# A four-layer vision network on one core: attention's keys in column groups, its first maxima earlier, and layer 2 begun with the values

## The chip, the cores and the metric

The kernel runs on one core of a Trainium2 chip, as one launch for a batch of four images. The metric is the device time of the launch in microseconds (us); lower is better. Each time below is that of the whole launch.

## The reference

Four images of 256 channels and 64 x 64 points pass through four layers one after the other; each layer adds its output to its input, and reads its input normalised over groups of 8 channels:

```python
x = x + deform_conv(gn(x))      # layer 0: 3x3 deformable convolution
x = x + attention(gn(x))        # layer 1
x = x + dcnv4(gn(x))            # layer 2
x = x + mamba(gn(x))            # layer 3: a selective scan
```

Two of the layers matter here. Layer 1, with N = 4096 points:

```python
q = xf @ Wq.T + bq              # 32 channels
k = xf @ Wk.T + bk              # 32 channels
v = relu(xf @ Wv.T + bv)        # 128 channels
attn = softmax(q @ k.T)         # 4096 x 4096 for each image
comb = (attn @ v) @ Wc.T + bc
out = concatenate([comb, v])
```

Layer 2 samples a value map `xp = x @ w_value + b_value`, padded by one point, at nine learned offsets for each of 16 groups, weighs the samples with a learned mask, and projects the sum:

```python
val = w00*g(y0,x0) + w01*g(y0,x0+1) + w10*g(y0+1,x0) + w11*g(y0+1,x0+1)
out = einsum('bhwkgc,bhwgk->bhwgc', val, mask)
```

## The kernel before

The input `x` of one image stays in SBUF as 2 x 128 channels on 128 partitions, and all four layers work on it in place. The images follow one another; in each of them the layers follow one another, since a layer's normalisation needs the statistics of the whole image. The order of a stage's instructions is written out by hand for the engines that `tc.manual_schedule` names; for the other engines, and for the DMA queue of SyncE (SP), a planner orders the instructions from its own estimate of when each will be ready. Within an engine instructions run strictly in that order.

**Layer 1 (`layer1`).** `scaled` (L186, VectorE) writes the normalised input `xn` in sixteen pieces of 128 x 512. Then comes a part that is called the front here (L485 to L519), in which only TensorE's order is by hand. It goes over eight chunks `j` of 512 points. For each chunk three products of 128 x 512 are made: values `pv`, keys `pk`, queries `pq` (all on L499; each is two matrix products over 128 channels, and each of these is two instructions[...]). The weights of keys and queries hold the same 32 columns four times side by side, so that the 32 rows of `pq` and of `pk` stand on all four groups of 32 partitions. Queries are kept that way in `qa` (L506). Of the keys, a chunk keeps one group of 32 rows only (L505): chunk `j` goes to the partitions of group `j % 4` and to half `j // 4` of `ka`, so that later four products with a contraction of 32 rows run in the four row groups of the array at once. The values are turned into rows of points by four transposes (`pvt`, L509) and kept in `v`; they are also added to `x` (L516), and the next layer's statistics of that chunk are taken (L152).

The softmax subtracts each query's greatest score before the exponential. `greatest(qb, wide, n)` finds the greatest of all 4096 scores for each of the 512 queries of block `qb`. It makes 32 score tiles of 128 x 512 (L455), `n` at a time into one PSUM tile, and reduces them with VectorE (L465); a generator's `yield` after each step lets the caller place it in TensorE's order. Then it splits the maxima into three bf16 parts (L472 to L475), turns them into a row with four small products (`pmt`, L479), and copies the row to SBUF (`mr`, L483). In the front it is called for block 0 with `n = 2` and two PSUM tiles of two banks: after each odd chunk four steps, and after the last chunk also the closing part. In the attention loop behind it (`scores`, `weigh`) it is called with `n = 3` for the blocks 1 to 7, each while the block before is worked on. The loop starts with `scores(0)`, which needs the row of block 0; its exponentials are L544.

**Layer 2 (`layer2`).** `scaled` writes the normalised input into `xr` (L186 again, 20 pieces of 256 to 512 columns), laid out as two halves of the image side by side. The loop then goes over 16 pairs of rows `p`. The values of rows are held in a ring of four tiles (`ring`, 128 x 2560, L690 to L692): `values(q)` makes two rows of values with TensorE (`pc`, L702 and L704), copies them into the middle of ring tile `q % 4` with ScalarE (L705), and lets eight DMAs of SP's queue copy them, shifted by one and two columns to either side, into the four other places (L709). Places at the image's edge that no DMA writes must be zero, so GpSimd clears each ring tile at the layer's start (L691). `offsets` (L720, L723) makes offsets and mask, `hats`, `masked` and `outer` make bilinear weights from them, `clear` and `gather` add these into a table `A` of 5 x 5 weights, `product` (L823) multiplies the ring with it, and `total` (L840) sums on TensorE. Row `p` needs ring tiles `p` to `p + 2`. From the line `with tc.manual_schedule` in `layer2` on, the order is by hand for TensorE, ScalarE, VectorE and GpSimd; the four clearings of the ring stand ahead of it, so the planner places them.

Of the kernel before, what the change touches and what calls it, by code (L numbers as in the profile page):

```python
# [9 lines left out]
F32 = mybir.dt.float32  # L10
I32 = mybir.dt.int32
BF16 = mybir.dt.bfloat16
AF = mybir.ActivationFunctionType
ALU = mybir.AluOpType
AX = mybir.AxisListType

P = 128
# [42 lines left out]
WIN = 5  # L60
VR = 2


class Net:
# [346 lines left out]
    def layer1(self, x):  # L411
# [4 lines left out]
        with tc.tile_pool(name="l1a", bufs=1) as pa, tc.tile_pool(name="l1b", bufs=2) as pb:  # L416
# [24 lines left out]
            def greatest(qb, wide, n):  # L441


                m8 = pb.tile([P, 4, 8], F32, tag="m8", name="m8")
                m = m8.rearrange("p t m -> p (t m)")
                if n == 2:
                    units = [(t, c, g) for c in range(2) for h in range(2) for t in range(4) for g in (2 * h, 2 * h + 1)]
                else:
                    units = [(t, c, g) for t in range(4) for c in range(2) for g in range(4)]
                for u in range(0, 32, n):  # L450
                    now = units[u : u + n]
                    sc = wide("pm")
                    for i, (t, c, g) in enumerate(now):
                        r = slice(32 * g, 32 * g + 32)
                        nc.tensor.matmul(  # L455
                            sc[:, i, :],
                            qa[r, bass.ts(4 * qb + t, P)],
                            ka[r, bass.ts(c, 512)],
                            start=True,
                            stop=True,  # L460
                            tile_position=(32 * g, 0),
                        )
                    t, c, g = now[0]
                    at = 8 * t + 4 * c + g
                    nc.vector.tensor_reduce(m[:, at : at + len(now)], sc[:, : len(now), :], AX.X, ALU.max)  # L465
                    yield
                mx = pb.tile([P, 4], F32, tag="mx", name="mx")
                nc.vector.tensor_reduce(mx, m8, AX.X, ALU.max, negate=True)
                mp = parts[qb % 2]
                for i in range(3):  # L470
                    t3 = pb.tile([P, 4], BF16, tag="t3", name="t3")
                    nc.scalar.copy(t3, mx)  # L472
                    nc.scalar.copy(mp[:, :, :, i], t3.rearrange("p (t u) -> p t u", u=1).to_broadcast([P, 4, 4]))
                    if i < 2:
                        nc.vector.tensor_sub(mx, mx, t3)  # L475
                yield
                pt = wide("pmt")[:, 0, :]
                for t in range(4):
                    nc.tensor.matmul(  # L479
                        pt[:, bass.ts(t, P)], mp[:, t].rearrange("p g r -> p (g r)"), identb, start=True, stop=True  # L480
                    )
                mr = pb.tile([P, 512], BF16, tag="mr", name="mr")
                nc.vector.tensor_copy(mr, pt)  # L483
                rows.append(mr)

            with (
                tc.manual_schedule(engines={mybir.EngineType.PE}),
                self.banks(4, "l1p") as pone,
                self.banks(2, "l1w") as ptwo,
            ):  # L490
                pair = lambda name: ptwo.tile([P, 2, 512], F32, tag="pm", name=name)
                one = lambda name: pone.tile([P, 512], F32, tag="p", name=name)
                ahead = greatest(0, pair, 2)
                for j in range(NCH):
                    to = {}
                    for n, w in (("v", wv), ("k", wk), ("q", wq)):
                        to[n] = one("p" + n)
                        for ct in range(2):
                            nc.tensor.matmul(  # L499
                                to[n], w[:, ct, :], xn[:, ct, bass.ts(j, 512)], start=(ct == 0), stop=(ct == 1)  # L500
                            )
                    vt = pb.tile([P, 512], F32, tag="vt1", name="vt1")
                    nc.vector.tensor_scalar(vt, to["v"], bv, 0.0, ALU.add, ALU.max)
                    r = slice(32 * (j % 4), 32 * (j % 4) + 32)
                    nc.scalar.activation(ka[r, bass.ts(j // 4, 512)], to["k"][r, :], AF.Identity, bias=bk[r])  # L505
                    nc.scalar.activation(qa[:, bass.ts(j, 512)], to["q"], AF.Identity, bias=bq)  # L506
                    pt = one("pvt")
                    for i in range(4):
                        nc.tensor.transpose(pt[:, bass.ts(i, P)], vt[:, bass.ts(i, P)], self.ident)  # L509
                    nc.scalar.copy(v[:, 4 * j : 4 * j + 4, :].rearrange("p t c -> p (t c)"), pt)  # L510

                    if j % 2:
                        for _ in range(4):
                            next(ahead)
                    xs = x[:, 1, bass.ts(j, 512)]
                    nc.vector.tensor_add(xs, xs, vt)  # L516
                    self.note(x, 1, j)
                next(ahead)
                next(ahead, None)  # L519

            blocks = [{} for _ in range(NCH)]
# [131 lines left out]
    def layer2(self, x):  # L653
# [5 lines left out]
        with (  # L659
# [28 lines left out]
            for i in range(4):  # L688

                r = pa.tile([P, WIN, VR, 256], F32, tag=f"ring{i}", name=f"ring{i}")  # L690
                nc.gpsimd.memset(r, 0.0)  # L691
                ring.append(r)  # L692

            def values(q):
# [156 lines left out]
            with tc.manual_schedule(  # L851
                engines={
                    mybir.EngineType.PE,
                    mybir.EngineType.Activation,
                    mybir.EngineType.DVE,
                    mybir.EngineType.Pool,
                }
            ):
                for t in range(T):
                    offsets(0, t)  # L860
                hats(0, 0)
                hats(0, 1)
                clear(0)
                values(0)
                masked(0)
                for i in range(3):
                    outer(0, i, nc.gpsimd if i == 1 else nc.vector)
                values(1)
                values(2)
                for t in range(T):  # L870
                    offsets(1, t)
                for i in (0, 2, 1):
                    gather(0, i)
                hats(1, 0)
                hats(1, 1)


                behind = None
                for p in range(last + 1):
                    near, far = p < last, p < last - 1  # L880
                    for wy in range(WIN):
                        product(p, wy, 0)
                        if near and wy == 0:
                            masked(p + 1)
                        product(p, wy, 1)
                        if wy == 1 and p > 1:
                            finish(p - 2)
                        if near and wy > 1:
                            gather(p + 1, wy - 2)
                        if near and wy < 3:  # L890
                            outer(p + 1, wy, nc.gpsimd)
                        prod = pairs(p)
                        if behind:
                            total(*behind)
                        behind = p, wy, prod
                        if wy == 0:
                            if near:
                                clear(p + 1)
                            if p:
                                nc.scalar.copy(made[p - 1]["o"].rearrange("p t c -> p (t c)"), made[p - 1]["pd"])  # L900
                        if far and wy < 2:
                            offsets(p + 2, wy)
                        if wy == 2:
                            if far:
                                hats(p + 2, 0)
                            if p < last:
                                values(p + 3)
                        if wy == 3:
                            if far:
                                hats(p + 2, 1)  # L910
                            if p:
                                turned(p - 1)
                        if wy == 4 and p:
                            project(p - 1)
                total(*behind)
                nc.scalar.copy(made[last]["o"].rearrange("p t c -> p (t c)"), made[last]["pd"])
                finish(last - 1)
                turned(last)
                project(last)
                finish(last)  # L920
# [710 lines left out]
```

## Time and profile before

| what | value |
|---|---|
| median of the runs shown | 10109.86 us (10098.28 to 10119.21) |
| the profiled execution | 10144.41 us, of which its span is 10142.6 us |
| mean granted TensorE clock | 0.95 of full speed |
| TensorE busy | 8738.3 us, 86% of the span |
| VectorE busy | 7651.8 us, 75% |
| GpSimd busy | 6768.8 us, 67% |
| ScalarE busy | 4961.6 us, 49% |

In the first image the stages that matter lie as follows (us from the span's start). The others look the same, some 2500 us apart.

| stage | from | to | length |
|---|---|---|---|
| front of layer 1, from the first piece of `xn` to the first exponential | 634.2 | 713.3 | 79.1 |
| attention loop, first to last exponential | 713.3 | 1148.3 | 435.0 |
| end of layer 1 and start of layer 2, to the first product with the ring | 1148.3 | 1198.2 | 49.9 |
| layer 2's loop | 1198.2 | 1545.7 | 347.5 |

Busy shares are means over stages with different limits. What an edit in one stage is worth is read from that stage: from who waits for whom in it, and from which wait ends last.

### The profile page before, as it was taken

How to read it: one execution, taken by the hardware profiler on the slowest of the kernel's cores; microseconds unless marked ns; L12 is line 12 of the kernel's file. 1: busy time of each engine (PE TensorE's matmuls, PEld its weight loads, DVE VectorE, ACT ScalarE, POOL GpSimd, SP SyncE). 2: the span in 40 equal slices, each digit the busy share in tenths (PEclk: the TensorE clock that was granted, in tenths of full speed). 3: DMA queues.
4: the chain of work that ended last, by engine and by line, in shares of the span. 5: the costliest groups of instructions: out<-in, count | busy, mean ns of one | idle time of the engine just before them, and what ended most of it. 6: DMA issues, size and time to landing. Idle time of an engine off the chain costs nothing.

```text
span 10142.6 us, 88824 instructions
## 1 busy us (share of the span) xinstructions
PE 8738.3 (86%) x29189; PEld 4281.7 (42%) x29193; DVE 7651.8 (75%) x8215; ACT 4961.6 (49%) x7588; POOL 6768.8 (67%) x3952
## 2 busy tenths in 40 slices
PE   5789898998678989899877898989986789998997
PEld 3643343333464334333346434433334643443333
DVE  5764497999676459799967545889995754688998
ACT  3743334665474333566557333266645733326664
POOL 3646686787474668688757366768865736677886
PEclk9889999999899999999989999999998999999999
DMA  7830011111783001111178201111118810111111
GB/s 263 310 137 1 25 49 39 44 45 48 259 312 119 1 29 49 38 44 47 45 287 323 78 1 36 51 38 44 44 43 316 308 62 1 38 49 38 40 40 34
DMA packets 377891, 956.56 MB, mean 94 GB/s; under 512 B 34675, under 2 KB 107820, under 8 KB 375372
## 3 DMA queue, kind: packets, MB, share of 16 engines
q0 software_dynamic: 165888, 604.05, 16.6%
q1 hardware_dynamic: 211532, 346.73, 10.8%
q8 instruction: 234, 3.83, 0.2%
q14 instruction: 237, 1.94, 0.1%
HBM read 784.59 MB, written 92.32 MB: 86 GB/s over the span
## 4 chain that ended last, share of the span: by engine, by line
PE 24%; DVE 9%; ACT 5%; issue 4%; POOL 4%; DMA 3%; another core or an unknown queue 1%; SPq 0%; POOLq 0%; DVEq 0%; ACTq 0%
PE cx L555 5%; DVE h L1476 4%; PE pacc L840 3%; PE y L1388 2%; DMA g<-tab,idx 2%; PE pm L455 2%; PE front L1236 2%; POOL h L1490 2%; DVE h L1468 2%; PE sc L531 2%; PE front L1190 1%; ACT da L1475 1%; DVE r L353 1%; POOL g L344 1%; DMA ring<-ring 1%
## 5 line engine op out<-in xcount | busy, mean ns | idle before, releaser
L1476 DVE TENSOR_TENSOR_SCAN h<-da,carry,h 128x512 f32<-128x512 f32 x2048 | 2470.6, 1264 | 140.9 <-ACT da L1475 92.5
L1490 POOL TENSOR_TENSOR h<-h,cn 128x2048 f32<-128x2048 f32 x508 | 2300.0, 4527 | 41.1 <-POOL carry L1487 0.4
L1475 ACT ACTIVATE da<-delta,l3a 128x512 f32<-128x512 f32 x2048 | 1388.6, 689 | 1152.5 <-DVE h L1476 1150.7
L1388 PE MATMUL y<-h,ident 128*128 128x512 f32 x4096 | 1931.4, 616 | 4.5 <-POOL h L1490 3.5
L344 POOL DMA_INDIRECT g<-tab,idx x1152 | 1363.3, 1183 | 791.1 <-issue 362.8
L548 POOL TENSOR_TENSOR acc<-acc,e 128x1024 f32<-128x1024 f32 x480 | 1125.1, 2344 | 540.4 <-ACT e L544 519.7
L388 PE MATMUL pz<-cols,l0w 128*128 128x256 f32 x4608 | 1217.5, 411 | 219.8 <-ACT cols L377 95.8
L1388 PEld LDWEIGHTS y<-h,ident 128*128 128x128 f32 x4096 | 810.2, 198 | 1279.3 <-issue 1209.7
L353 DVE SCALAR_TENSOR_TENSOR r<-g,wx,r 128x512 f32<-128x512 f32 x1152 | 858.1, 745 | 434.3 <-ACT r L352 321.9
L1468 DVE TENSOR_TENSOR h<-du,bn 128x2048 f32<-128x2048 f32 x512 | 1157.9, 2262 | 26.3 <-PE front L1190 14.2
L465 DVE TENSOR_REDUCE m<-pm 128x3 f32<-128x1536 f32 (+1 forms) x372 | 602.3, 1625 | 716.9 <-PE pm L455 715.2
L388 PEld LDWEIGHTS pz<-cols,l0w 128*128 128x128 f32 x4608 | 896.9, 205 | 390.7 <-ACT cols L377 100.9
L823 DVE TENSOR_TENSOR prod<-ring,A 128x1280 f32<-128x1280 f32 x640 | 922.4, 1480 | 122.7 <-DMA ring<-ring 102.7
L555 PE MATMUL cx<-e,v 128*128 128x512 f32 x2048 | 1001.4, 616 | 0.0
L544 ACT ACTIVATE e<-sc 128x1024 f32<-128x1024 f32 x512 | 496.0, 1020 | 1032.4 <-PE sc L531 1032.4
L352 ACT ACTIVATE r<-g,wx 128x512 f32<-128x512 f32 x1152 | 826.6, 718 | 270.0 <-DMA g<-tab,idx 219.2
L840 PE MATMUL pacc<-prod,ident 128*128 128x512 f32 x1920 | 915.3, 610 | 37.7 <-DVE prod L823 23.7
L832 POOL TENSOR_TENSOR prod<-prod 128x512 f32<-128x512 f32 x640 | 800.3, 1274 | 187.8 <-DVE prod L823 170.1
L370 PE MATMUL pt<-ident,acc 128*128 128x128 f32 x2304 | 430.9, 295 | 304.9 <-DVE acc L361 200.7
L1487 POOL COPY carry<-h 128x4 f32<-128x4 f32 x512 | 98.0, 191 | 807.4 <-DVE h L1476 797.6
L555 PEld LDWEIGHTS cx<-e,v 128*128 128x128 f32 x2048 | 352.2, 189 | 598.8 <-issue 596.3
L360 ACT ACTIVATE acc<-r,wy 128x256 f32<-128x256 f32 x1152 | 571.4, 496 | 28.0 <-DVE r L353 22.4
(250 smaller groups left out, 11138.0 us busy)
## 6 DMA issues: line engine op xcount, KB each, us to landing
cn<-cd SPq DMA_DIRECT2D x512, 256.0 KB
tab<-vt SPq DMA_DIRECT2D x112, 640.0 KB
ring<-ring SPq DMA_DIRECT2D x288, 126.0 KB
ring<-ring SPq DMA_DIRECT2D x288, 124.0 KB
g<-tab,idx POOLq DMA_INDIRECT x1152
x<-in_x SPq DMA_DIRECT2D x64, 256.0 KB
out<-x SPq DMA_DIRECT2D x56, 256.0 KB
l0w<-in_l0w SPq DMA_DIRECT2D x4, 2304.0 KB
```

The costliest lines, as they stand in the source:

```text
L344: nc.gpsimd.indirect_dma_start(out=g[:], out_offset=None, in_=tab[:, :], in_offset=bass.IndirectOffsetOnAxis(ap=idx[:, t, k : k + 1], axis=0),
L353: nc.vector.scalar_tensor_tensor(r, g[:, :, 1, :], wx[:, 1, t, k : k + 1], r, ALU.mult, ALU.add)
L388: nc.tensor.matmul(sums[m][:, ot, :256], wf[:, i, bass.ts(ot, P)], cols[m][:, i, :], start=(i == 0), stop=(i == 17),)
L548: nc.gpsimd.tensor_add(b["acc"], b["acc"], e)
L555: nc.tensor.matmul(blocks[qb]["cx"], v[:, 4 * (i + kt // 4 * 4) + kt % 4, :], e[:, bass.ts(i % 2, 512)], start=(kt == 0 and i == 0), stop= ...
L823: nc.vector.tensor_mul(d["prod"][:, :, t, :].rearrange("p x (g c) -> p x g c", c=GC), ring[y // VR % 4][:, :, y % VR, :].rearrange("p x (g ...
L840: nc.tensor.matmul(d["pd"], self.ident, prod[:, wx, :], start=(wy == 0 and wx == 4), stop=(wy == WIN - 1 and wx == 2),)
L1388: nc.tensor.matmul(c["ys"][dc], self.ident, h[:, dc, :], start=False, stop=(n == DS - 1))
L1468: nc.vector.tensor_mul(h, c["du"], c.pop(("bn", n)).to_broadcast([P, 4, C]))
L1475: nc.scalar.activation(da, c["delta"][:, dc, :], AF.Exp, scale=al[:, dc, n : n + 1])
L1476: nc.vector.tensor_tensor_scan(h[:, dc, :], da, h[:, dc, :], carry[:, dc, n : n + 1], ALU.mult, ALU.add)
L1490: nc.gpsimd.tensor_mul(h, h, cn.to_broadcast([P, 4, C]))
```

## The change

In layer 1's front, the keys of four chunks are made together: `keys(c)` takes only 32 columns of the weights and lets four products run side by side in the four column groups of the array, each writing its own 32 partitions of one PSUM tile; one copy of 128 x 512 then fills half of `ka`. The maxima of block 0 are made four tiles at a time (one PSUM tile of four banks in place of two of two banks), in the same order as in the loop, and they are placed between the chunks from chunk 1 on, with the closing part in chunks 6 and 7. A small exponential of a constant (`tiny1`) stands ahead of the front. In layer 2 GpSimd clears ring tiles 0 and 1 at the start, ScalarE clears tile 2, and GpSimd clears tile 3 inside the hand-written order; `values(0)` stands ahead of the first `offsets`, `values(1)` ahead of the first `masked`, and `values(2)` behind the second pair of `offsets`.

```diff
--- before.py
+++ after.py
@@ -443,10 +443,7 @@
 
                 m8 = pb.tile([P, 4, 8], F32, tag="m8", name="m8")
                 m = m8.rearrange("p t m -> p (t m)")
-                if n == 2:
-                    units = [(t, c, g) for c in range(2) for h in range(2) for t in range(4) for g in (2 * h, 2 * h + 1)]
-                else:
-                    units = [(t, c, g) for t in range(4) for c in range(2) for g in range(4)]
+                units = [(t, c, g) for t in range(4) for c in range(2) for g in range(4)]
                 for u in range(0, 32, n):
                     now = units[u : u + n]
                     sc = wide("pm")
@@ -486,36 +483,56 @@
             with (
                 tc.manual_schedule(engines={mybir.EngineType.PE}),
                 self.banks(4, "l1p") as pone,
-                self.banks(2, "l1w") as ptwo,
+                self.banks(1, "l1w") as pfour,
             ):
-                pair = lambda name: ptwo.tile([P, 2, 512], F32, tag="pm", name=name)
+                four = lambda name: pfour.tile([P, 4, 512], F32, tag="pm", name=name)
                 one = lambda name: pone.tile([P, 512], F32, tag="p", name=name)
-                ahead = greatest(0, pair, 2)
+
+                tiny = pa.tile([P, 1], F32, tag="tiny1", name="tiny1")
+                nc.scalar.activation(tiny, self.eps, AF.Exp)
+
+                def keys(c):
+
+                    pk = one("pk")
+                    for ct in range(2):
+                        for g in range(4):
+                            nc.tensor.matmul(
+                                pk[32 * g : 32 * g + 32, :],
+                                wk[:, ct, :32],
+                                xn[:, ct, bass.ts(4 * c + g, 512)],
+                                start=(ct == 0),
+                                stop=(ct == 1),
+                                tile_position=(0, 32 * g),
+                            )
+                    nc.scalar.activation(ka[:, bass.ts(c, 512)], pk, AF.Identity, bias=bk)
+
+                def project(n, w, j):
+                    to = one("p" + n)
+                    for ct in range(2):
+                        nc.tensor.matmul(to, w[:, ct, :], xn[:, ct, bass.ts(j, 512)], start=(ct == 0), stop=(ct == 1))
+                    return to
+
+
+                ahead = greatest(0, four, 4)
                 for j in range(NCH):
-                    to = {}
-                    for n, w in (("v", wv), ("k", wk), ("q", wq)):
-                        to[n] = one("p" + n)
-                        for ct in range(2):
-                            nc.tensor.matmul(
-                                to[n], w[:, ct, :], xn[:, ct, bass.ts(j, 512)], start=(ct == 0), stop=(ct == 1)
-                            )
+                    pv = project("v", wv, j)
                     vt = pb.tile([P, 512], F32, tag="vt1", name="vt1")
-                    nc.vector.tensor_scalar(vt, to["v"], bv, 0.0, ALU.add, ALU.max)
-                    r = slice(32 * (j % 4), 32 * (j % 4) + 32)
-                    nc.scalar.activation(ka[r, bass.ts(j // 4, 512)], to["k"][r, :], AF.Identity, bias=bk[r])
-                    nc.scalar.activation(qa[:, bass.ts(j, 512)], to["q"], AF.Identity, bias=bq)
+                    nc.vector.tensor_scalar(vt, pv, bv, 0.0, ALU.add, ALU.max)
+                    if j > 1:
+                        next(ahead, None)
+                    pq = project("q", wq, j)
+                    nc.scalar.activation(qa[:, bass.ts(j, 512)], pq, AF.Identity, bias=bq)
+                    if j < 2:
+                        keys(j)
+                    if j in (1, 3, 5, 6):
+                        next(ahead)
                     pt = one("pvt")
                     for i in range(4):
                         nc.tensor.transpose(pt[:, bass.ts(i, P)], vt[:, bass.ts(i, P)], self.ident)
                     nc.scalar.copy(v[:, 4 * j : 4 * j + 4, :].rearrange("p t c -> p (t c)"), pt)
-
-                    if j % 2:
-                        for _ in range(4):
-                            next(ahead)
                     xs = x[:, 1, bass.ts(j, 512)]
                     nc.vector.tensor_add(xs, xs, vt)
                     self.note(x, 1, j)
-                next(ahead)
                 next(ahead, None)
 
             blocks = [{} for _ in range(NCH)]
@@ -688,7 +705,12 @@
             for i in range(4):
 
                 r = pa.tile([P, WIN, VR, 256], F32, tag=f"ring{i}", name=f"ring{i}")
-                nc.gpsimd.memset(r, 0.0)
+                if i < 2:
+                    nc.gpsimd.memset(r, 0.0)
+                elif i == 2:
+                    nc.scalar.copy(
+                        r.rearrange("p x y c -> p (x y c)"), zero.to_broadcast([P, WIN * VR * 256])
+                    )
                 ring.append(r)
 
             def values(q):
@@ -856,19 +878,20 @@
                     mybir.EngineType.Pool,
                 }
             ):
+                values(0)
                 for t in range(T):
                     offsets(0, t)
                 hats(0, 0)
                 hats(0, 1)
                 clear(0)
-                values(0)
+                values(1)
                 masked(0)
                 for i in range(3):
                     outer(0, i, nc.gpsimd if i == 1 else nc.vector)
-                values(1)
-                values(2)
                 for t in range(T):
                     offsets(1, t)
+                nc.gpsimd.memset(ring[3], 0.0)
+                values(2)
                 for i in (0, 2, 1):
                     gather(0, i)
                 hats(1, 0)
```

## The prediction

> **What bounds the kernel now.** I read the page first: TensorE is busy for 86% of the span and no other engine for more than 75%, but these are means, so I went to the stages. The view of busy time by stretches, for the front of layer 1, the attention loop, the start of layer 2 and layer 2's loop (length, then busy time of PE, PEld, DVE, ACT and POOL, granted clock, DMA share, GB/s):
>
> ```profile
> 634.20:713.30 79.10, 73.52 (x208) 30.74 (x208) 44.98 (x61) 17.19 (x31) 0.00 (x0) 0.87 0.00 0
> 713.30:1148.30 435.00, 424.21 (x1915) 164.25 (x1916) 176.25 (x133) 136.57 (x177) 285.64 (x127) 0.99 0.00 1
> 1148.30:1198.20 49.90, 33.48 (x92) 17.27 (x90) 23.76 (x42) 12.60 (x17) 16.40 (x13) 0.69 0.16 51
> 1198.20:1545.70 347.50, 334.74 (x935) 161.37 (x936) 318.41 (x352) 107.04 (x164) 274.82 (x203) 0.99 0.16 49
> ```
>
> The front is TensorE's, at 0.87 of its clock; the start of layer 2 is nobody's. The chain of waits, in order of time, shows the front of image 4 (start, length, what):
>
> ```profile
> 8191.28 1.11 PE pm L455 x4
> 8192.41 1.24 DVE m L465
> 8193.69 1.13 PE pm L455 x4
> 8194.82 1.13 PE pm L455 x4
> 8195.95 1.92 PE pv L499 x4
> 8197.87 1.72 PE pk L499 x4
> 8199.58 1.72 PE pq L499 x4
> 8201.30 0.44 PE pvt L509 x4
> ```
>
> So the path runs through every projection, 1.72 us each, and passes to VectorE only where four steps of maxima come at once. The same view at the start of layer 2, image 3:
>
> ```profile
> 6190.72 3.22 PE pom L720 x4
> ...
> 6201.06 0.72 ACT A L756
> 6201.78 0.52 ACT ring L705
> ...
> 6209.31 9.35 DMA ring<-ring
> 6218.67 12.36 DMA ring<-ring
> 6231.05 12.21 DMA ring<-ring
> ```
>
> Offsets come first, then ScalarE's weights, then the copy of `values(0)`, and three ring tiles' DMAs, one after the other. What comes ahead of that is in the order of time of image 1 (start, length, what):
>
> ```profile
> 1160.53 8.88 POOL L691 MEMSET ring<- 128x2560 f32 x4
> 1165.79 4.46 DVE L186 TENSOR_SCALAR xr<-x,gm,rs 128x256 f32<-128x256 f32 x4
> ```
>
> Four pieces of `xr` take 4.46 us, although a piece of 128x512 takes 533 ns in the table by shape: the clearing lies over them, and ends at 1169.41.
>
> [...] layer 0's convolution in this form (L280) issues 144 instructions in 15.66 us, 0.109 us each, against 0.43 us for one of `pk`. [...] The first two pieces above end only with the third and the fourth clearing. [...] The front's clock records show windows of 3.41 us at 0.50: one behind each of the first two groups of four maxima, two behind the third. [...] Ring DMAs have 62 or 63[...]; the 62-row ones follow each other at 2.5 us in the trace's landings, and a ring tile takes 12.2 us.
>
> **Part 1, layer 1's front, per image.** From the first `pv` (634.84) to the first exponential (713.31): 78.5 us.
> - Keys: 8 x 4 x 0.43 = 13.8 us become 2 x 16 x 0.109 = 3.5. On TensorE's path: -10.3. ScalarE's eight copies (678 ns) become two of some 688 ns (the row of `qa`), hidden beside TensorE.
> - Maxima: 16 steps of 0.86 us (two of the four row groups at work) become 8 of 0.97 (the loop's eight instructions of `sc` start 0.97 ahead of what follows). -6.0.
> - VectorE's waits inside the four groups: four steps take 4.67 us in the chain above, for 3.44 of matmul. -1.2 x 4 = -4.9.
> - Half clock behind them: four windows of 3.41 us, half lost. -6.8.
> - The tail: after the last maxima (four steps, ending at 708.4) the row of block 0 still needs the split, `pmt` and `mr`, 4.9 us to the first exponential. Now the row is ready ahead of it; `scores(0)` waits for the last copies of `qa` and `v`, and takes 1.3: 2.5 in all. -2.4.
> - New waits: the PSUM tile of four banks is single, so a step waits for the reduction before it. By 1024 in 1.22 and 1536 in 1.757 us, 2048 take 2.3. Between most steps TensorE has 3.9 us of other work; behind it are queued the next projections, and the chunk's transposes wait in turn for VectorE's `vt`. In chunks 3 and 5, with two steps each, only `pq` (1.72) lies between: some 1.35 us each; with 0.35 in four other places and 0.5 for `pmt`, +4.6. One of these stops may cost a window at half clock: +1.7, taken half, 0.9.
> VectorE has 7.4 (`xn`) + 8 x 2.15 + 8 x 2.3 + 1 = 44 us of work in it, TensorE 31.0 + 3.5 + 7.8 + 0.3 = 42.6 and a cold start of 2.9: both nearly full, the new length some 53 us. Sum: 30.4 - 5.5 = **-25**. Bounds: -30 if the new waits vanish; -17 if VectorE's order, which the planner sets, puts sums and statistics ahead of reductions and each step stops for another microsecond. The little exponential only moves a table load of 1.28 us; the old one was hidden by `mr`. If the planner puts it ahead of the square root, the load returns beside the last `v` copy: 0 to +1.3, taken 0.
>
> **Part 2, start of layer 2, per image.** T is the first ring DMA: 1181.48 in image 1, 15.7 us after the first piece of `xr` (1165.79); 16 to 17 in the others.
> - The clearing: two memsets (2.23 each) from 1160.53 end at 1165.0, ahead of `xr`. `values(0)` needs the first two pieces: 0.4 each (20 pieces without the overlap follow at 0.46), so TensorE starts near 1166.4.
> - `values(0)`: two rows at the half clock, 2.3 each as at 1181.5, 4.7; copy and hand-over 0.8. T becomes 1171.9: **-9.6**, and some 10 over the four images.
> - Behind it on TensorE the first offsets start 4.7 later than their pieces allow, near 1171 against 1170.03, so `hats` hardly move. ScalarE has `hats` and the clear of `A` ahead of the copy of `values(1)`, so that comes near 1181.5, T + 9.6, where before the ninth DMA went out at T + 7.3. The two engines then still have rows until T + 16.3: hidden. `values(2)` stands behind `offsets(1)`, which waits for `masked(0)` to free its banks, near 1180.5; the copy comes near 1191, T + 19, as before (1200.38). All eight DMAs of each tile keep their order on SP's queue, and the queue is bound by the 62-row transfers, so all three tiles land earlier by the shift of T.
> - `gather(0)` ends near 1188.5, level with tile 0; the products before tile 1 have 3 us to spare.
> - ScalarE's clear: 800 elements take 842 ns (`A`), so 2560 some 2.7 us, between 1160.6 and the square root's load at 1163.92. Cover 0.6 us; if the planner puts it late, at most 2.7 on the path of `rs`. GpSimd's clear of tile 3 (2.23) lies between its `outer` and its first `pairs`, which waits for tile 0: hidden, and without that cover 2.2.
> Bounds: -11.5 to -5. Layer 2's loop is TensorE's from the third tile on, so the shift stays. In both parts removed work cannot slow TensorE's order itself; a loss could come only through the clock or the planner, below.
>
> **Sum.** 4 x 25 + 4 x 10 = 140 us. The profiled execution would go from 10144.4 to 10004; it lies 34 us above the median, and I take the difference off the median: 10109.86 - 140 = **9970**.
>
> **Rivals.**
> 1. *VectorE sets the front's pace* (13%): every step stops TensorE for a reduction and what the planner put ahead of it. For it: 44 us of work on VectorE in a front of 53. Against it: the loop does just this with three tiles, stops 0.8 us a step, and keeps a clock of 0.99. At -12 an image, with layer 2's 10, -88: 10022.
> 2. *Layer 2's start gains only part* (9%): tile 2 comes late because of `values(2)`, or the clearing of tile 2 delays the square root. At -3 an image: 9998.
> 3. *The column groups do not overlap* (3%): the change does not do what it says of the keys, 2 x 16 x 0.43 = 13.8 as before. Against it is L280. -15 and -10 an image: 10010.
> 4. *Slower* (3%): the front falls to half clock and stays there, since each of eight steps ends in a full stop of 2.3 us on the single PSUM tile. 42.6 x 2 + 18.4 + 2.5 = 106 us, +28 an image, less 10: 10182. It decides from a front of 89 us on. The clock fell behind each group of maxima before; but those used half the row groups, and the loop's stops never lowered it.
>
> **How the numbers follow.** The likeliest case has 72%. The bounds, 4 x (17 to 30) and 4 x (5 to 11.5), give -88 to -166, 9944 to 10022. They hold rivals 2 and 3 and the edge of 1. I say 9942 to 10020. About 0.2%, 20 us, is what a measurement of this kernel can tell from no change: faster 0.95, same 0.02, slower 0.03.
>
> **What would show it.** Right: the front takes 50 to 58 us; `po`-like products of `pk`, 32 instructions at 0.11 us; eight reductions of 128x2048 at 2.3 us; no gap between the last `pvt` and `sc` but for a copy; the first pieces of `xr` at 0.4 us each; the first ring DMA 6 us after them, and three tiles still at 12.2 us each. Wrong: a front over 65 us with a clock below 0.85 (step of new waits), or a third tile that lands less than 6 us sooner after `xr` (part 2).

## The result, and the profile after

| what | before | after |
|---|---|---|
| median | 10104.07 us (4 runs, 10093.64 to 10119.21) | 9973.85 us (4 runs, 9971.41 to 9981.35) |
| ratio | 1 | 0.9871, 95% interval 0.9854 to 0.9888 |
| profiled execution | 10144.41 us (span 10142.6) | 9981.35 us (span 9979.5) |

The change saves 130.2 us, where 140 were forecast. In one of 25 executions of the kernel before, in a later series, the granted clock was 0.82 and the time 10876.27 us; medians and ratios below leave it out. The two profiled executions differ by 163.1 us of span, which is more than the change gives. Setting the stages of the four images against each other in the two traces:

| stage, sum over four images | before | after | difference |
|---|---|---|---|
| front of layer 1, first `xn` to first exponential | 314.2 | 228.0 | -86.2 |
| attention loop and its end | 1783.8 | 1785.5 | +1.7 |
| last addition of layer 1 to the product that waits for the third ring tile | 253.0 | 209.4 | -43.6 |
| rest of layer 2 and start of layer 3 | 1574.4 | 1583.4 | +9.0 |
| the rest of layers 0 and 3, and the end | 6217.1 | 6173.2 | -43.9 |

The two stages that were edited give -129.8, the difference of the medians. The last row has no edited line in it; over all the traces of this study, of whatever kernel, it lies between 6173.2 and 6230.9 us, so a difference of 43.9 is within what one trace differs from another. Nearly all of the +9.0 is a window at half clock of 10.2 us that falls at layer 3's start in two of the four images of this trace, at 4.2 us each; another execution of the same kernel has it in one.

The view of busy time by stretches after the change, image 1 (length, then busy time of PE, PEld, DVE, ACT and POOL, granted clock, DMA share, GB/s), the same four stages as before:

```profile
619.90:676.80 56.90, 49.83 (x208) 19.42 (x208) 43.55 (x53) 13.46 (x25) 0.00 (x0) 0.95 0.00 0
676.80:1112.00 435.20, 424.82 (x1915) 164.48 (x1916) 176.23 (x133) 136.59 (x178) 285.59 (x127) 0.99 0.00 1
1112.00:1152.60 40.60, 32.34 (x92) 16.15 (x90) 20.70 (x43) 12.50 (x16) 19.88 (x12) 0.75 0.21 66
1152.60:1498.50 345.90, 333.95 (x936) 161.74 (x935) 318.35 (x352) 109.25 (x166) 274.81 (x203) 0.98 0.16 49
```

In the front PE falls by 24 us at the same count of instructions (208), VectorE's work stays (44.98 to 43.55), and the clock rises from 0.87 to 0.95. The loops keep their lengths within 2 us. The groups by shape in that front (line, engine, operation, shapes, count, busy, mean ns, idle before), maxima and keys before, and then after the change:

```profile
L455 PE MATMUL pm<-ka,qa 32*128 32x512 f32 x64 | 18.0, 659 | 2.0 <-DVE m L465 2.0
L499 PE MATMUL pk<-xn,l 128*128 128x512 f32 x32 | 17.1, 662 | 0.0
```

```profile
L462 DVE TENSOR_REDUCE m<-pm 128x4 f32<-128x2048 f32 x8 | 18.2, 2280 | 5.0 <-PE pm L452 5.0
...
L452 PE MATMUL pm<-ka,qa 32*128 32x512 f32 x64 | 9.1, 639 | 3.4 <-DVE m L462 3.2
L499 PE MATMUL pk<-xn,l 128*32 128x512 f32 x32 | 3.8, 598 | 0.0
L561 ACT ACT_TABLE_LOAD x1 | 1.3, 1283 | 1.5 <-issue 1.5
```

32 instructions of keys in four column groups have TensorE busy for 3.8 us, where the 32 before took 17.1: a mean of 598 ns each, yet 0.12 us apiece, since four run side by side. The 64 of maxima take 9.1 instead of 18.0. The reduction of four banks takes 2.28 us. The last line is the load of ScalarE's function table between the first scores and the first exponential, on the path. Before, it ran beside `mr`, to 712.64, and the exponential came at 713.31:

```profile
711.36 1.28 ACT L544 ACT_TABLE_LOAD   x1
711.90 0.69 DVE L483 CAST mr<-pmt 128x512 bf16<-128x512 f32 x1 [1.09 <-PE pmt L479]
```

The chain of waits at the start of layer 2, image 4 (start, length, what):

```profile
8549.65 2.32 ACT ring L711
8551.99 1.28 ACT L175
...
8553.85 0.42 DVE xr L186
...
8554.52 2.04 PE pc L724 x4
...
8556.89 1.80 PE pc L724 x4
...
8558.99 0.59 ACT ring L727
...
8566.22 10.09 DMA ring<-ring
8576.32 12.29 DMA ring<-ring
8588.63 12.22 DMA ring<-ring
```

Offsets, hats and the clearing of `A`, which stood in the chain before, are gone from it: one piece of `xr`, two rows of values, one copy, and then the DMAs, still 12.2 us a tile. ScalarE's own clearing stands at its head. The groups by shape around it, image 1:

```profile
L186 DVE TENSOR_SCALAR xr<-x,gm,rs 128x256 f32<-128x256 f32 x4 | 1.4, 408 | 0.1
L709 POOL MEMSET ring<- 128x2560 f32 x2 | 4.4, 2231 | 0.0
L1078 POOL TENSOR_SCALAR l3a<-l3a 128x64 f32<-128x64 f32 x1 | 6.1, 6117 | 2.4 <-ACT l3a L1077 2.4
```

Nothing lies over the pieces of `xr` now, so four take 1.4 us in place of 4.46.

### The profile page after: what moved, and what is told of

It is laid out like the page before. It is cut to its first block, busy times and chain, and to the rows that moved or that the text cites. A ratio compares the mean times of both kernels' runs of the same rounds, so it can differ in the third digit from the quotient of the medians.

```text
span 9979.5 us, 88756 instructions
## 1 busy us (share of the span) xinstructions
PE 8624.9 (86%) x29193; PEld 4231.9 (42%) x29193; DVE 7632.5 (76%) x8183; ACT 4959.9 (50%) x7576; POOL 6758.0 (68%) x3948
## 5 line engine op out<-in xcount | busy, mean ns | idle before, releaser
L462 DVE TENSOR_REDUCE m<-pm 128x3 f32<-128x1536 f32 (+2 forms) x340 | 599.3, 1763 | 699.7 <-PE pm L452 699.7
L561 ACT ACTIVATE e<-sc 128x1024 f32<-128x1024 f32 x512 | 496.0, 1020 | 1029.7 <-PE sc L548 1029.7
L845 DVE TENSOR_TENSOR prod<-ring,A 128x1280 f32<-128x1280 f32 x640 | 922.6, 1480 | 79.1 <-DMA ring<-ring 60.8
```

The costliest lines, as they stand in the source:

```text
L845: nc.vector.tensor_mul(d["prod"][:, :, t, :].rearrange("p x (g c) -> p x g c", c=GC), ring[y // VR % 4][:, :, y % VR, :].rearrange("p x (g ...
```

## The experiments

Each was measured beside the kernel before: the first four on one chip, the next four on a second, the last four on a third. The kernel before had medians of 10136.55, 10116.06 and 10144.68 us there, so totals are compared on one chip, or as ratios. The changed kernel was run on the third of these chips alone: on the first two it stands only by its ratio of the first measurement, 0.9871 (0.9854 to 0.9888), and against it differences below some 20 us can't be told by time. Stage times are sums over four images in the profiled execution, worked out from the starts in the trace.

**Each part alone.** The changed kernel with layer 2 as before:

```diff
-                values(0)
                 for t in range(T):
                     offsets(0, t)
...
-                values(1)
+                values(0)
                 masked(0)
...
+                values(1)
+                values(2)
                 for t in range(T):
                     offsets(1, t)
-                nc.gpsimd.memset(ring[3], 0.0)
-                values(2)
```

(and all four clearings on GpSimd, as before).

> Layer 1's part of the change alone, layer 2 as before. If the two parts are independent, the front shortens by some 21.5 us an image as in the profile of the whole change, so 86 us less than before, some 10018, and layer 2's start keeps its 63 us. If the parts need each other, or if a part of the 130 us came from layer 0 (whose transfers differ from run to run), it lies above 10035.

10045.07 us, ratio 0.9909 (0.9896 to 0.9923): -91.5, where 86 were expected; that the time itself is above the 10035 is this chip's, on which the kernel before takes 32 us more than in the first measurement. Front 227.4 us; start of layer 2 253.4, as before.

And the kernel before with layer 2's edits only, the same lines the other way round:

> Layer 2's part of the change alone, layer 1 as before. Independent parts: 11 us an image between the last addition of layer 1 and the product that waits for the third ring tile, 44 us in all, some 10060. If the windows at half clock at the start of layer 3, which two of four images showed in the profile of the whole change and none before, come with the shift of layer 2, up to 9 us of that are lost: 10069.

10092.25 us, ratio 0.9951 (0.9937 to 0.9965): -44.3. Front 315.8, start of layer 2 208.2. The start of layer 3 shows no long window here (70.9 to 71.6 us in the four images), so the shift of layer 2 alone need not bring it. The two parts add up to 135.8, against 139.2 for both together on the third chip (below) and 130.2 in the first measurement: they are independent within what the times can tell.

**Keys alone.** The kernel before with keys in four column groups; maxima in pairs, at their old places:

```diff
-                    for n, w in (("v", wv), ("k", wk), ("q", wq)):
+                    for n, w in (("v", wv), ("q", wq)):
...
+                    if j < 2:
+                        keys(j)
```

> Only the keys: made for four chunks in four column groups in chunks 0 and 1; the maxima of block 0 stay in pairs, four steps behind each odd chunk, and the tail stays. By the prediction's sum this takes 10.3 us an image off TensorE's order and leaves the 4.9 of waits, the 6.8 of half clock and the tail: -41 us, some 10063, a front of 68.5 us with three or four windows at half clock. Rival: with less work between the groups of maxima the clock falls more often, so that the gain is below 8 us an image.

10101.33 us, ratio 0.9968 (0.9956 to 0.9980): -35.2; front 275.2, so -39.0, or 9.8 an image. Stretches, image 1, of this front, and then of the run with the whole front:

```profile
624.00:693.60 69.60, 64.06 (x208) 25.32 (x208) 45.00 (x61) 13.13 (x25) 0.00 (x0) 0.84 0.00 0
```

```profile
623.30:680.20 56.90, 49.73 (x208) 19.41 (x208) 43.55 (x53) 13.51 (x26) 0.00 (x0) 0.95 0.00 0
```

With keys alone the clock is even lower than before, 0.84, but the windows at half clock are as many as before, four of 3.41 us in image 1, and stand where the groups of maxima are; the rival's fall of the clock did not come. They go with the early maxima of four tiles, which take the other 12 us of an image (275.2 to 227.4 over four). TensorE was not idle ahead of these windows: in the 3.41 us before each run of them in the front, in every image of the kernel before, it was busy for 2.9 us, with maxima and at most one other instruction. That a stop of TensorE brings such a window, on which the prediction's 0.9 us and its rival 4 rested, was the author's assumption, and these windows do not show it. The change does two things to these maxima at once: it has four row groups at work in place of two, and it breaks up the groups of four steps. Which of the two removes the windows was not tried.

**The table load.** The changed kernel with its small exponential reading `xn`, so that it comes behind the square root:

```diff
-                nc.scalar.activation(tiny, self.eps, AF.Exp)
+                nc.scalar.activation(tiny, xn[:, 0, 0:1], AF.Exp)
```

> The whole change, but the little exponential reads the first piece of xn in place of the constant, so that it can't run ahead of the square root. Theory: in the changed kernel its table is displaced by the square root's, and the load of 1.28 us stands between the first scores and the first exponential, behind a wait; here it moves into ScalarE's idle time at the front's start, 1.3 us less an image, 5 us below the changed kernel (9969), and a front of 55.6 us. Rival: the load is not on the path (the row or the PSUM copy ends last), no change within 0.05%. If the window at half clock at the start of the loop comes from this stop, it goes as well, another 1 to 2 us an image.

Front 221.9 us, 6.1 less than 228.0: 1.5 an image. The total, 9986.96 us, has ratio 0.9857 (0.9841 to 0.9873), which does not part from the changed kernel's 0.9871. The window at half clock at the start of the loop, which the expectation suspected of the load, stays in all four images (3.4 to 6.8 us). Table loads by shape, of the changed kernel and then of this one, from layer 0's end to the first exponentials:

```profile
L492 ACT ACT_TABLE_LOAD x1 | 1.3, 1283 | 2.9 <-PE pz L388 2.9
L175 ACT ACT_TABLE_LOAD x1 | 1.3, 1283 | 2.9 <-PE pv L173 2.9
L561 ACT ACT_TABLE_LOAD x1 | 1.3, 1283 | 1.5 <-issue 1.5
```

```profile
L175 ACT ACT_TABLE_LOAD x1 | 1.3, 1283 | 7.5 <-PE pv L173 7.5
L492 ACT ACT_TABLE_LOAD x1 | 1.3, 1283 | 0.9 <-DVE xn L186 0.9
```

In the changed kernel three loads are made: the planner put `tiny1`, which waits for nothing late, ahead of the square root (L175), which loads its own table over it; the exponential (L561) pays again, on the path. With an input that comes late there are two, and none at L561.

**Order without spread.** The changed kernel with all four clearings on GpSimd ahead of `xr`:

```diff
-                if i < 2:
-                    nc.gpsimd.memset(r, 0.0)
-                elif i == 2:
-                    nc.scalar.copy(
...
+                nc.gpsimd.memset(r, 0.0)
...
-                nc.gpsimd.memset(ring[3], 0.0)
```

> The changed kernel with all four clearings of ring tiles put back on GpSimd ahead of the first normalized value; the values still come before the offsets. My theory: of layer 2's gain of 10.9 us an image, the order gives most and the spread of the clearing only part. With four clearings GpSimd is at work for some 13 us, so the pieces of the normalized array on VectorE run beside it (2.6 us instead of 0.41 for the first), and ScalarE has nothing between the exponential and the square root, so the 1.28 us table load stands on the path again: from the last addition of layer 1 to the product that waits for the third ring tile 52.3 us grow to some 56 to 57, 16 to 20 us over the changed kernel for four images, still 24 to 28 us under the kernel before in this stretch. Rival: the spread is what gives the gain (the values would have been held up by the clearing anyway): then nearly all of the 44 us are lost. Second rival: the clearing is hidden, and the time is that of the changed kernel within 5 us.

9996.50 us, ratio 0.9882 (0.9867 to 0.9898), which the times alone do not part from the changed kernel; the stretch (from the last addition of layer 1 to the product that waits for the third ring tile) 222.1, 12.7 more than the changed kernel, somewhat less than the 16 to 20 expected. The four clearings take 8.9 us, not the 13 of the expectation. The chain of image 4:

```profile
8574.42 1.28 ACT L175
8576.28 3.77 DVE xr L186 x2
8580.19 1.19 PE pc L719 x2
8581.71 2.00 PE pc L719 x4
```

Two pieces of `xr` take 3.77 us on the path. The price an image is 2.4 us there (8.45 from first piece to first ring DMA, against 6.0) and 0.9 ahead of it (5.97 from the last addition to the first piece, against 5.0 to 5.3).

**Spread without order.** The kernel before with the clearing spread only; its diff is the corresponding part of the change.

> The kernel before with the clearing of the ring's tiles spread alone: tile 2 on ScalarE, tile 3 on GpSimd later; the offsets stay ahead of the values. My theory: the pieces of the normalized array come some 3 us earlier and the square root's table load may slip out of the path (1.3 us), but the offsets ahead of the values still take their time, so the stretch from the last addition to the third tile's product falls from 63.2 to some 59 us an image: about 12 to 17 us less than the kernel before. Together with the run that has the order alone the two should give about 44 us. Rival: the order of the instructions is all, and the spread gives nothing (0 to 3 us).

10093.52 us (21 runs), ratio 0.9978 (0.9971 to 0.9984): -22.5; the stretch 235.9, 17.1 less than before. The chain of image 4, where the offsets still come first:

```profile
8658.33 3.13 PE pom L725 x4
...
8663.71 1.22 ACT hat L740
8664.93 1.05 ACT hat L741
...
8668.52 0.72 ACT A L761
8669.24 0.52 ACT ring L710
```

Order alone saves 253.0 - 222.1 = 30.9, the spread alone 17.1, both 43.6: the order gives more, but each is worth something without the other, and none of the rivals in the two expectations holds. Singly they sum to 48.0, so 4.4 of it is gained by either one.

**What sets the ring's 12.2 us.** The changed kernel with each transfer of 62 rows cut in two:

```diff
-                        nc.sync.dma_start(out=r[a:b, 2 + d, :, :], in_=r[a + d : b + d, 2, :, :])
+                        for c0, c1 in ((a, a + 60), (a + 60, b)) if abs(d) == 2 else ((a, b),):
+                            nc.sync.dma_start(out=r[c0:c1, 2 + d, :, :], in_=r[c0 + d : c1 + d, 2, :, :])
```

> The changed kernel with each ring transfer of 62 rows cut into 60 rows and 2 rows. In the changed kernel a ring tile's four copies end 12.2 us after each other, and the theory puts this down to the 62-row transfers[...]. If so, the third tile lands some 15 to 25 us earlier, and the stretch from the last addition of layer 1 to its product (52.3 us an image) gets shorter by 4 to 10 us until the next thing ends last (the gather's offsets and weights, or the values of tile 2 on TensorE at half clock): 15 to 40 us less in all, and up to 10 us more at the end of layer 2 where the last rows' copies are waited for. Rival: the queue of the issuing engine or what comes after it sets the pace (eight more issues a tile row at some 0.7 us each): no gain, or some us slower.

9951.00 us, ratio 0.9841 (0.9826 to 0.9857); the stretch 176.1, 33.3 less than the changed kernel or 8.3 an image. The DMA view in 40 slices, busy share of the 16 engines in tenths and GB/s, of the changed kernel (1130 to 1175 us) and of this one (1135 to 1165 us):

```profile
DMA  0000012443421111344321111124541111111111
GB/s 0 0 0 0 7 16 80 102 144 87 126 78 51 51 51 51 118 144 157 115 75 51 51 51 49 46 67 153 171 162 66 51 51 51 66 49 53 51 49 36
```

```profile
DMA  0000040413444633200140414444615040404444
GB/s 0 0 0 0 0 158 11 137 33 117 131 137 142 199 131 112 57 0 0 46 123 36 134 33 156 128 145 139 224 46 156 0 164 5 161 19 139 131 153 134
```

The plateaus at 51 GB/s are the 62-row transfers (124 KB at one landing in 2.5 us are 51 GB/s); in the second view they are gone. From 1144 to 1148 us, in the first plateau, the engines' share is 13.2%, the time of 2.1 of the 16; over the whole of the two views it is 21.0% in the first and 28.8% in the second. On how many engines one transfer lies is not shown. The issuing queue did not set the pace, though it has four issues more for each ring tile (four of the eight transfers have 62 rows; the expectation's eight is wrong). The products with the ring, in the costliest groups of the page, changed kernel and then this one:

```profile
L845 DVE TENSOR_TENSOR prod<-ring,A 128x1280 f32<-128x1280 f32 x640 | 922.6, 1480 | 79.1 <-DMA ring<-ring 60.8
```

```profile
L846 DVE TENSOR_TENSOR prod<-ring,A 128x1280 f32<-128x1280 f32 x640 | 919.7, 1481 | 40.2 <-PE pacc L863 37.6
```

DMAs no longer end most of VectorE's waits for these products; TensorE does. At the start of layer 2 VectorE now waits for ScalarE's hats, made from the offsets (image 1: total, times, longest):

```profile
DVE mh L769 <- ACT hat L762: 9.6, 2, 6.6
```

So what the change put behind `values(0)` ends last there, as the expectation named it. Whether another order is better with cut transfers was not tried. The hoped-for gain at the loop's end didn't come: from the third tile's product to the last one takes 323.0 us in image 1, as with uncut transfers (323.1). The waits for the last rows there were off the path.

**An addition on GpSimd.** The changed kernel with the front's `x` additions moved from VectorE:

```diff
-                    nc.vector.tensor_add(xs, xs, vt)
+                    nc.gpsimd.tensor_add(xs, xs, vt)
```

> The changed kernel with the eight additions of the front (x plus the attention values) on GpSimd, which is idle there, instead of VectorE. VectorE is at work for 43.6 of the front's 56.9 us, and two maxima in chunks 3 and 5 wait for it for some 0.4 us each beyond the spacing of 1.07. If VectorE's load makes these stalls, the front gets shorter by 0.8 to 2 us an image (3 to 8 us in all, about what can be measured). Rival: [...] the additions cost more on GpSimd than they free: the last one stands ahead of the first scores' operands, so the front gets longer by 1 to 3 us an image. Second rival: nothing moves, since the stalls are TensorE's own.

9989.97 us, ratio 0.9878 (0.9863 to 0.9893), not parted from the changed kernel by time; front 238.1, 10.1 longer, or 2.5 an image, which is a length that the first rival gave (1 to 3). But the trace shows a wait that no theory had named:

```profile
DVE st L152 <- POOL x L534: 10.0, 8, 1.4
```

(waits in image 1's front: total, times, longest). The addition takes 1.26 us on GpSimd instead of 0.69, and the chunk's statistics, which VectorE takes in order ahead of other work, wait for it eight times. The reductions behind them come later, and TensorE's stops for reductions grow from 3.2 to 4.4 us in image 1 (its front from 56.9 to 58.2). Work was taken off VectorE, but the wait stayed in its queue. Statistics and reductions themselves take as long as before (0.69 and 2.28 us), so nothing shows VectorE held up; since it stands idle for most of each addition (10.0 of 10.1 us), whether the two engines would hold each other up can't be told from this run.

**The changed kernel again, and VectorE's order.** First the changed kernel on the third chip:

> The changed kernel itself once more, so that the kernels beside it can be set against it on one chip. 0.985 to 0.989 of the kernel before. The front is 56.3 to 57.4 us an image and the stretch from the last addition of layer 1 to the third ring tile's product 52.3 us, as in its first profile.

10005.47 us, ratio 0.9867 (0.9852 to 0.9882): -139.2; front 227.2, stretch 209.4. Beside it, the changed kernel with VectorE's front in the written order:

```diff
-                tc.manual_schedule(engines={mybir.EngineType.PE}),
+                tc.manual_schedule(engines={mybir.EngineType.PE, mybir.EngineType.DVE}),
```

> The changed kernel with VectorE's instructions of the front kept in the written order too. In the changed kernel the planner puts the addition and the statistics of a chunk (0.69 us each) ahead of the maxima's reduction, which is 1.2 us late by it in chunks 3, 5 and 6; the next maxima find their one buffer of four banks taken, which is the 1.50 us idle time seen twice in an image. In the written order the reduction goes first. My theory: the two idle times fall from 1.50 to some 0.6 us (a maxima unit and its reduction, 1.07 and 2.28 and a handover, against 2.92 us of maxima and projection), and the last row of maxima comes 0.8 us earlier: front 2 to 2.6 us shorter an image, 8 to 10 us in all. Rival: the addition and statistics then delay VectorE's next copy of the values by 1.4 us, the transposes behind it wait, and the front stays as it is or grows by up to 1 us an image.

Front 217.6, 9.6 less than beside it, as the theory had it. TensorE's waits for the reductions in image 1's front, of the changed kernel and then of this one:

```profile
PE pm L452 <- DVE m L462: 3.2, 3, 1.5
```

```profile
PE pm L452 <- DVE m L462: 1.2, 3, 0.5
```

But the total is 10005.66 us (ratio 0.9866, 0.9851 to 0.9881), no gain at all. Layers 0 and 3 took 12.0 us more in this trace than in the one beside it, within the 58 us over which they vary. A gain of 9.6 in 10000 us stands in the trace and is below what the times resolve here; whether it reaches the total stays open.

**The best version.** The small exponential and the cut transfers together, and then with VectorE's order as well:

> The changed kernel with two edits together: the small exponential that reads the normalized array (table load off the path, 1.5 us an image) and the ring transfers of 62 rows cut into 60 and 2 (8.3 us an image). If the two are independent: 36 to 40 us less than the changed kernel on the same chip. Rival: the earlier run of the small exponential had no gain in total time; then 30 to 33 us.

> The two edits (small exponential, cut transfers) and VectorE's written order in the front. By the theory: 44 to 50 us less than the changed kernel on the same chip. By the rival of VectorE's order: as without it, 36 to 40 us, or less gain.

9966.41 us, ratio 0.9824 (0.9810 to 0.9837), for the first: 39.1 less than the changed kernel beside it, as expected of independent edits. 9967.84 us, ratio 0.9827 (0.9814 to 0.9840), for the second: 37.6 less, the same, where its theory had 44 to 50 and the rival 36 to 40; yet its front is shorter again (214.5 against 222.1). Either beats both kernels. The second is also the one trace of fourteen without a window at half clock at the start of the attention loop, in any of its four images; the loop and its end take 1779.4 us over four images there and 1781.7 to 1785.8 in the others. Both edits that shorten the stop ahead of the loop are in it, each of which alone leaves the window; that the shorter stop is the cause is not shown.

## Why the prediction was right, and where its sum was off

The mechanism held in both parts, and the sum was 10 us too large: 4 x 3.5 over in the front, 4 x 0.9 under in layer 2. That the forecast total, 9970, lies within 4 us of the measured 9973.85 is luck: the median from which the saving was taken, 10109.86, lay 6 us above the 10104.07 of the four runs. **Front: -21.5 us an image, forecast -25.** Term by term, image 1 where a single image is meant:

- *Keys*, forecast -10.3: keys alone give -9.8.
- *Maxima*, eight steps of 0.97: a step starts 1.07 ahead of what follows it, and the first instruction of a projection behind it takes 0.1 longer than others (0.53 to the next start against 0.43), as does the one ahead of it. Over eight steps, less the same at the four groups before, that is some 1.5 us more than forecast (an estimate from these starts). This is the first mis-sized term: the loop's spacing was taken over to other neighbours.
- *VectorE's waits and half clock in the groups*, -4.9 and -6.8: both gone; the only window at half clock in the front is the one at its start (6.8 us from 619.0). The 0.9 set aside for a new one was not needed.
- *New waits*, forecast +4.6: the stops come to some 4.8, 3.8 at the maxima and 1.0 at `pmt`.
- *Tail*, forecast 2.5 us and the table load at 0: the tail, from the last transpose to the first exponential, is 3.7. This is the step that failed. The text named the case (the planner puts the small exponential ahead of the square root, at most +1.3) and took zero without a reason. The load returned in full, 1.28, and the run without it gained 1.5 an image.

The forecast of -24.9 with +1.5, +0.2, +0.5 for keys, +1.2 for the tail and -0.9 gives -22.4; image 1 measured -22.2 (79.1 to 56.9). The mean over the four images is lower since the front of image 4 before was shorter (77.2, with three windows at half clock where the others have four).

*Rival 1* (VectorE sets the pace) did not come, but its mechanism is the larger of the two losses that the runs took out of the changed front: additions and statistics ahead of reductions stop TensorE for 1.50 us twice an image, and in the written order for at most 0.5 (2.4 us an image; the table load 1.5). Rivals 2 to 4 did not come either: the third tile moved with the first, the keys take 3.8 us, and the front's clock is 0.95.

**Start of layer 2: -10.9 us an image, forecast -10.** From the first piece of `xr` to the first ring DMA: 15.7 to 17.2 us before, 5.75 to 6.07 after; the text said 6. From there to the third tile's product it is 41.0 to 41.2 before and 41.1 to 41.6 after, so the three tiles did shift together, and `values(1)` and `values(2)` were hidden. Most of the 0.9 beyond the forecast lies ahead of `xr`, from the last addition to its first piece, 5.96 to 5.00 us in image 1: with ScalarE's clearing (2.32 us, estimated 2.7) the square root's table load runs straight behind it instead of after its wait for `pv`. The spread alone shows 5.0 too, and the order with all clearings on GpSimd 5.97; why the load waits in one case and not in the other was not tried.

The working that the ring is bound by the 62-row transfers was an argument ahead of the result, from their 2.5 us each; cutting them has shown it (33.3 us less).

## What to carry to other kernels

Cost an edit in the stage that it touches, and look for it in that stage: here unchanged layers vary by more from one execution to the next than some edits give. An instruction that is there to load a table early must have an input that stops the planner from putting it ahead of another table's user: here that left two of three loads of 1.28 us. And before moving work off a full engine, look at what in its queue reads the result: here the statistics waited there, in order, eight times and 10.0 us in one front.

## What the runs showed of the hardware

- Ring transfers of 62 rows ran at 51 GB/s, and cut into 60 and 2 they left no plateau: 8.3 us an image here, for one line.
- In the front before, windows at half clock came behind stretches of 3.41 us in which TensorE was busy for 2.9 us, nearly all of it with products of 32 rows in two of the four row groups, and went when these were made in four row groups, with other work between the steps.
- A small GpSimd operation (`l3a`, L1078 after), issued while VectorE writes the pieces of `xr`, took 6.12 us in image 1 and ended with the last piece; in the other three images it took 0.62 to 0.69 beside the same pieces, and 0.40 before, behind the clearings. The prediction had seen VectorE's pieces last longer under GpSimd's clearing (four in 4.46 us, and in 1.4 without it); in image 1 it is GpSimd's operation that lasts longer, and why in the others not is open. Nothing waited for it.
- Windows at half clock did not stand at fixed places of a kernel: layer 3's start took 74.9 and 74.8 us in images 1 and 3 and 70.6 in the others of one execution, and 74.9 in image 1 and 71.1 to 71.4 in the others of the next.
